# A semaphore for each place of gathered rows, and three and two sets in turn fetched by ScalarE

## The chip, the cores and the metric

The kernel runs on one core of one Trainium2 chip. The metric is the device time of one execution in microseconds (us); of several runs the median counts. The core has five engines with queues of their own: TensorE (PE; its weight loads are PEld), VectorE (DVE), ScalarE (ACT), GpSimd (POOL) and SyncE (SP, which only issues DMAs). Sixteen DMA engines carry out what ScalarE, SyncE and GpSimd issue. An engine works through its queue in order; engines wait for each other, and for DMAs, with semaphores.

## The reference

One layer of a graph network over N = 50,000 nodes with D = 160 features and E = 1,650,000 edges, sorted by destination (every node's edge to itself among them). Each edge takes the features of its source node, combines them with its four edge numbers through five small weight matrices, and adds the result to its destination; then follow two more weight matrices, a ReLU, two residual sums and a layer norm:

```python
s = x[:, :64]
v = x[:, 64:].reshape(n, 32, 3)
ss, vv = (s[src], v[src])
...
out0 = C0 * (ss * e0 @ W1 + dot * INV3 @ W2)
...
m_agg = jax.ops.segment_sum(m, dst, num_segments=n)
...
return x + jax.nn.relu(h)
...
x = _layernorm(x + _L0_gnn_ref(...), axis=-1)
```

Since everything up to the ReLU is linear in the gathered features, the kernel sums first (for each destination, the source rows weighted by each of the four edge numbers) and applies the joined weights once for each block of 128 nodes.

## The kernel before

**Tiling.** The edges are taken in sets of 128, one edge on each partition. Six sets (`G = 6`) make a group whose destinations lie in a window of `W = 32` nodes; two groups (`PG = 2`) make a pair, so a pair has 12 sets; ten pairs (`SG = 20` groups, 120 sets) make a superstep, called `s` in the code. The edges of a node to itself are taken out on the way (by the "packs", lines 594 to 758, of which there are 11) and added from rows read in order, so that 2,087 groups, 12,522 sets in 1,044 pairs and 105 supersteps are left.

**One set.** The 128 source rows of a set, 640 bytes each, come into a tile of 128x160. VectorE builds for a pair the operand `ha` (lines 483 and 486): for each edge a one-hot place in the window, times its four numbers. TensorE multiplies it with the rows (line 511), and the six sets of a group add up in PSUM. VectorE then turns the sums and adds them to a ring of node sums (lines 527 and 536). When a block of nodes is complete, TensorE applies the weights (line 831), VectorE adds the residual and takes mean and variance (lines 186 to 191), ScalarE takes the square root (line 196), VectorE finishes (lines 200 and 202), and SyncE stores. Blocks go two at a time.

**Three ways to get the rows of a set.**

- GpSimd's gather (`gather`, lines 461 to 471): one indirect DMA for a set, with 128 indices from the tile `si`. It writes its place in a tile `xg` of 12 places. The pool has four such tiles (line 235), so 48 places.
- ScalarE's fetches: 128 single DMAs of one row each, whose addresses it loads into registers 32 at a time from `line`, a list that VectorE makes (`list_rows`, lines 403 to 415). From superstep `SCALAR_FIRST = 6` on it fetches two sets of each superstep; the last superstep is left out. Their tiles come from a pool of one more than the largest number a superstep takes.
- SyncE's fetches, one set a superstep from `SYNC_FIRST = 8` on, made in the same way, besides all plain loads and stores.

`spots` (line 359) spreads the fetched sets evenly over a superstep. Their rows are issued in the ten pairs from pair `FBEGIN = 4` of the superstep before to pair 4 of their own, so many after each matmul of the code (`deal`, line 393), and a set is used `FWAIT = 4` pairs after its last row was due to be issued. Each fetched set has a semaphore out of a small ring of them, which its matmul waits for by hand.

**Semaphores of the gathers.** A gather has none by hand. The framework gives the gathers eight semaphores of its own in turn, and makes each gather wait until the one before it on the same semaphore, eight gathers earlier, has landed; the first eight have none to wait for. The first gather of a tile waits besides for the matmuls that read the tile's last contents, four tiles earlier, and has a separate semaphore instruction for what else it waits for. A matmul waits for the semaphore of its own gather.

**Order.** For SyncE, TensorE, VectorE and ScalarE the order is the order of the code (line 1009). In the main loop (lines 1011 to 1063) a pair's gathers are issued first; then come its 12 matmuls, and after the first of them the sums of the pair before are turned, after the third the operand of the next pair is built, and after each the fetchers issue their share and one step of the waiting work (blocks, packs, the next superstep's lists) is taken. The square root of two blocks is so handed over one pair after their sums, and what reads it one pair later. On ScalarE's queue the order is: the rows dealt so far, the square root, the next rows; and a few casts for the packs (lines 613 to 615 and 633).

Of the kernel before, what the change touches and what calls it, by code (L numbers as in the profile page):

```python
# [67 lines left out]
PG = 2  # L68
# [9 lines left out]
KM = WS - 1  # L78
REST = 15
LEAD = 3  # L80
BY_SCALAR, SCALAR_FIRST = (2,), 6
BY_SYNC, SYNC_FIRST = (1,), 8
FBEGIN, FWAIT = 4, 4

def plan(n_nodes, n_edges):

    nblk = 125
    assert n_nodes % nblk == 0
    assert W == FB
    nb = n_nodes // nblk  # L90
    again = 9

    per_unit = P * n_nodes / n_edges
    group = max(g for g in range(1, 17)
                if g == 1 or (g + 0.2) * per_unit + 1 + 5 * math.sqrt(g * per_unit * per_unit / P) <= W)
    head = math.ceil(min(HEAD, n_edges / (group * P)) / SG) * SG
    eh = head * group * P
    row = group * P * 3 // 2 + math.floor(per_unit * group * 3 / 2 * (1 - n_nodes / n_edges))
    assert row * n_nodes / n_edges + 5 * math.sqrt(row * n_nodes / n_edges / 16) < KM

    far = math.ceil(6 * math.sqrt(n_edges) / 2 * n_nodes / n_edges) + 2
    rows = math.ceil((n_edges - eh) / row) + 2
    ngroups = math.ceil((n_edges - n_nodes + eh * n_nodes / n_edges + far) / (group * P))
    assert eh + (rows - 1) * row - n_nodes + eh * n_nodes / n_edges - far >= ngroups * group * P
    units = P * math.ceil(max(math.ceil(n_edges / P) + again - 1, math.ceil((eh + rows * row + 1) / P)) / P)
    return nblk, nb, again, group, units, ngroups, row, head, rows, far
# [3 lines left out]
def tile_gnn_resnorm(ctx: ExitStack, tc: tile.TileContext, x, src, dst, attr, W1, W2, W3, W4, W5, Ws, Wv, out, n_edges):  # L110
    nc = tc.nc
    N = x.shape[0]
    NBLK, NB, GA, G, NU, NG, L, NH, NR, FAR = plan(N, n_edges)
# [95 lines left out]
    def near(g):  # L209
        p = g * G * P  # L210
        return p / degree if p <= EH else EH / degree + (p - EH) / (degree - 1)
# [6 lines left out]
    for g0, g1 in parts:  # L218
        t = min((near(g) / N for g in range(g0, g1 + 1)), key=lambda t: abs(t - 0.5))
# [14 lines left out]
    with tc.tile_pool(name="once", bufs=1) as once, tc.tile_pool(name="raw", bufs=2) as rawp, \  # L234
# [182 lines left out]
        def place(cast_):  # L417
# [40 lines left out]
            begun.append(nc.vector.tensor_reduce(extremes[:, 1, s:s + 1], rel[:, :n], axis=AX.X, op=ALU.max))  # L458
            placed[s] = si, rel, pk[:, :, us]

        def gather(s, placed, u, n):

            xg = rowp.tile([P, PG * G, D], F32, name="xg")
            rows = [fetched.pop((s, u + j), None) for j in range(n)]
            for j in range(n):
                if rows[j] is None:
                    rows[j] = xg[:, j, :], None, None, None
                    nc.gpsimd.indirect_dma_start(  # L468
                        out=xg[:, j, :], out_offset=None, in_=x,
                        in_offset=bass.IndirectOffsetOnAxis(ap=placed[0][:, u + j:u + j + 1], axis=0))  # L470
            return rows

        idle, sent = [], []
# [22 lines left out]
        def fresh(kind):  # L496
            written[kind].append([])

        def wrote(kind, ins):
            ws = written[kind]  # L500
            for old in ws[-3] if len(ws) > 2 else []:
                tc.declare_no_dep(ins.ins, old, reason="its reader has waited for it")
            ws[-1].append(ins.ins)
            return ins

        def group_sums(p, rows, ha):

            ps = psA.tile([P, PG, D], F32, name="ps")
            fresh("ps")
            for j, (xr, sem, count, key) in enumerate(rows):  # L510
                mm = nc.tensor.matmul(ps[:, j // G, :], ha[:, j].rearrange("p k w -> p (k w)"), xr,  # L511
                                      start=j % G == 0, stop=j % G == G - 1)
                if key:
                    mm.wait_op(sem, count, "sem-ge")
                    tc.declare_no_dep(mm.ins, group=key, reason="their own semaphore is waited for")
                    tc.declare_fence(mm.ins, group=key)
                if j % G == 0:
                    wrote("ps", mm)
                else:
                    written["ps"][-1].append(mm.ins)  # L520
                yield ps
# [22 lines left out]
        def row_start(r):  # L544

            lo, hi = (math.floor(r * L * (1 - 1 / degree)) - 2 * FAR - 2, math.ceil(r * L * (1 - 1 / degree)) + 2 * FAR + 2)
            return (max(lo, 0), hi if r else 0), (max(math.floor((EH + r * L) / degree) - FAR - 2, 0),
                                                  math.ceil((EH + r * L) / degree) + FAR + 2)
# [234 lines left out]
        def own_blocks(k):  # L783

            if min((k + 1) * S, N) <= row_start(0)[1][0]:
                return []
            return [list(range(b, min(b + BP, nblocks))) for b in range(k * SB, min((k + 1) * SB, nblocks), BP)]
# [196 lines left out]
        for i in range(npacks):  # L984
# [3 lines left out]
            own = next((k for k in range(NSEG) if min((k + 1) * S, N) > row_start(i * RP)[1][0] and own_blocks(k)), NSEG - 1)  # L988
# [22 lines left out]
        for p, (s, g, ng) in enumerate(pairs):  # L1011
# [5 lines left out]
            if p % per == 0 and s + 1 < NSC:  # L1017
                after_pair(p + 1, do_cast, s + 1)
                after_pair(p + 2, do_place, s + 1)
                if s + 2 == NSC:  # L1020
                    after_pair(p + 4, examine_all)
                    after_pair(p + 6, read_flags)
            rows = gather(s, placed[s], (g - s * SG) * G, ng * G)
            for j, ps in enumerate(group_sums(p, rows, has.pop(p))):
                if j == 1 and turning:
                    turn_sums(*turning)
                    turning = None
                if j == 3 and p + 1 < len(pairs):
                    s1, g1, ng1 = pairs[p + 1]
                    has[p + 1] = spread(placed[s1], (g1 - s1 * SG) * G, ng1 * G)  # L1030
                work(1.0)
                if p % per == FBEGIN and not j:
                    begun_at = p
                    for f in fetchers:
                        f.begin(s)
                for f in fetchers:
                    if f.left:
                        f.deal((p - begun_at + (j + 1) / (ng * G)) / per)
                if packs and p >= START:
                    when = p + (j + 1) / (ng * G)  # L1040
                    todo = math.ceil(len(packs[0]) * min(1, (when - began) / max(1, due[0] - began)))
                    for step in packs[0][done:todo]:
                        if step:
                            step()
                    done = max(done, todo)
                    if done == len(packs[0]):
                        packs.pop(0), due.pop(0)
                        done, began = 0, when
# [35 lines left out]
    with tc.tile_pool(name="up", bufs=1) as up, tc.tile_pool(name="us", bufs=2) as us, tc.For_i(0, once_more, 1):  # L1084
# [3 lines left out]
        mm = up.tile([P, 2, JU], F32, name="mm")  # L1088
# [32 lines left out]
        f = up.tile([PB, CB], F32, name="f")  # L1121
# [12 lines left out]
    with tc.tile_pool(name="edges2", bufs=2) as ep, tc.tile_pool(name="ops2", bufs=2) as op, \  # L1134
            tc.tile_pool(name="node2", bufs=1) as np_, tc.tile_pool(name="psA2", bufs=2, space=PSUM) as psA, \
            tc.tile_pool(name="psF2", bufs=1, space=PSUM) as psF:
        with tc.For_i(0, blocks, 1) as b:
# [5 lines left out]
            with tc.For_i(u0, u1, GA) as u:  # L1143
# [10 lines left out]
                xg = op.tile([P, GA, D], F32, name="xg2")  # L1154
# [71 lines left out]
```

## Time and profile before

| | us |
|---|---|
| median of 3 runs | 15441.45 |
| the runs | 15405.63, 15441.45, 15442.74 |
| the profiled execution, its own time | 15404.57 |
| its span, from the first instruction to the last | 15402.8 |

The granted TensorE clock of the profiled execution is 0.578 of full speed. The queues as the page has them (packets, MB, share of 16 engines):

```profile
q0 software_dynamic: 587040, 1002.66, 27.9%
q1 hardware_dynamic: 266794, 315.98, 6.7%
q10 hardware_dynamic: 51440, 17.04, 0.6%
```

The first is GpSimd's; the 25,088 row fetches of ScalarE and 12,288 of SyncE, and the plain loads and stores, are in the others.

How to read it: a row of the groups has line, engine, operation, what it writes and reads, the count, then busy time in us and the mean ns of one, then the idle time of that engine just before these instructions and what ended most of it. "issue" means that the profile shows nothing that was waited for. Instructions that issue DMAs, load registers or wait for semaphores are not counted as busy, so the share of an engine that mostly issues says little; in a view by time such instructions carry the engine's name with a q (ACTq). A view by time has start, duration, engine, line, operation, and in brackets the idle time before and what ended it. A row of the view of one line's instructions ends with the shortest, median and longest duration in ns and the first and last start in us. A row of a view by stretches has the stretch, its length, then busy time and count of PE, PEld, DVE, ACT and POOL, then the granted clock, the share in which the 16 DMA engines were busy, and GB/s.

### The profile page before, as it was taken

Reading aid. Unit: us, or ns where it says so; the run is one execution under the profiler, and the core shown is the slowest. Engines: PE = TensorE matmul, PEld = TensorE weight load, DVE = VectorE, ACT = ScalarE, POOL = GpSimd, SP = SyncE. Lnnn points to the kernel's source line nnn. Section 1 sums busy time; section 2 is a strip of 40 time slices with the busy share of each in tenths; the row PEclk is TensorE's granted clock in tenths of the full one; section 3 lists DMA queues with packets and bytes.
Section 4 is the critical chain, followed back from the end, with each engine's and each line's share of the span. In section 5 each row is a group of like instructions: output and inputs, shape, how many; then the busy total and the mean of one; then the engine's idle time right before and its main releaser. Section 6 shows DMA issues by size and latency. Waiting matters only on the chain.

```text
span 15402.8 us, 171527 instructions
## 1 busy us (share of the span) xinstructions
PE 10200.3 (66%) x28971; PEld 6755.8 (44%) x28972; DVE 7650.5 (50%) x12616; ACT 171.3 (1%) x273; POOL 11597.4 (75%) x12243
## 2 busy tenths in 40 slices
PE   3666666666666666666666666666666666666666
PEld 3444444444444444444444444444444444444444
DVE  8455355445535543563465355445634553554333
ACT  0000000000000000000000000000000000000000
POOL 7777777777777777777777777777777777777777
PEclk6655555555555555555555555555555555555555
DMA  3333333333333333333333333333333333333333
GB/s 83 100 81 94 91 81 85 97 88 83 92 94 81 84 96 91 81 85 98 87 83 91 93 82 84 97 88 82 86 98 87 81 88 93 81 86 85 86 81 75
DMA packets 906388, 1346.70 MB, mean 87 GB/s; under 512 B 291294, under 2 KB 680162, under 8 KB 902614
## 3 DMA queue, kind: packets, MB, share of 16 engines
q0 software_dynamic: 587040, 1002.66, 27.9%
q1 hardware_dynamic: 266794, 315.98, 6.7%
q10 hardware_dynamic: 51440, 17.04, 0.6%
q14 instruction: 883, 7.23, 0.2%
q8 instruction: 231, 3.78, 0.1%
HBM read 1263.28 MB, written 71.42 MB: 87 GB/s over the span
## 4 chain that ended last, share of the span: by engine, by line
POOL 53%; issue 23%; DMA 19%; PE 5%; DVE 1%; POOLq 0%
POOL xg L468 53%; DMA xg<-in_x,si 19%; PE ps L511 4%; PE phb L831 0%; DVE ha L486 0%; DVE ring L822 0%; DVE ring L536 0%; DVE sums L527 0%; DVE xr L818 0%; DVE hot L483 0%; DVE prow L697 0%; DVE ring L781 0%; DVE pri L692 0%; DVE spots L590 0%; DVE marks L690 0%
## 5 line engine op out<-in xcount | busy, mean ns | idle before, releaser
L468 POOL DMA_INDIRECT xg<-in_x,si x12230 | 11593.9, 948 | 3782.0 <-issue 3511.0
L511 PE MATMUL ps<-xg,ha 128*128 128x160 f32 x24460 | 9452.6, 501 | 5187.1 <-DMA xg<-in_x,si 4721.5
L511 PEld LDWEIGHTS ps<-xg,ha 128*128 128x128 f32 x24460 | 5773.0, 292 | 8629.5 <-DMA xg<-in_x,si 7467.8
L527 DVE STREAM_TRANSPOSE sums<-ps 128x320 f32<-128x320 f32 x1044 | 536.4, 514 | 6840.4 <-PE ps L511 6817.2
L486 DVE TENSOR_TENSOR ha<-hot,pk 128x1536 f32<-128x1536 f32 x1044 | 1830.5, 1753 | 35.9
L831 PE MATMUL phb<-BWk,ring 128*128 128x160 f32 (+1 forms) x3910 | 1256.1, 418 | 0.0
L831 PEld LDWEIGHTS phb<-BWk,ring 128*128 128x128 f32 (+1 forms) x3910 | 1027.4, 296 | 0.0
L536 DVE TENSOR_TENSOR ring<-ring,sums 128x160 f32 x2087 | 684.6, 328 | 340.1 <-issue 203.6
L483 DVE TENSOR_TENSOR hot<-bank,rel 128x384 f32<-128x384 f32 x1044 | 573.4, 549 | 12.6 <-DMA xt<-in_x 10.8
L697 DVE COPY_PREDICATED prow<-marks,prow 128x2370 f32<-128x2370 int32 (+5 forms) x198 | 548.6, 2771 | 1.1
L822 DVE STREAM_TRANSPOSE ring<-xr 128x1280 f32<-128x1280 f32 x188 | 467.4, 2486 | 6.5
L697 DVE COPY_PREDICATED pra<-marks,pra 128x1580 f32<-128x1580 int32 (+5 forms) x198 | 377.0, 1904 | 0.0
L818 DVE TENSOR_TENSOR xr<-xr,bank 128x1280 f32<-128x1280 f32 x188 | 278.9, 1484 | 6.6 <-DVE bank L817 0.2
L186 DVE SCALAR_TENSOR_TENSOR y<-phb,xt 128x320 f32<-128x320 f32 x196 | 95.5, 487 | 240.6 <-PE phb L831 240.3
L196 ACT ACTIVATE rstd<-mv,eps_t 128x2 f32<-128x2 f32 x196 | 58.0, 296 | 14076.2 <-DVE mv L191 13455.5
L533 DVE TENSOR_TENSOR ring<-ring 128x196 f32<-128x196 f32 (+20 forms) x485 | 149.0, 373 | 1.8
L511 PE MATMUL ps<-xscalar,ha 128*128 128x160 f32 x392 | 140.4, 460 | 0.0
L202 DVE TENSOR_SCALAR o<-y,mv,rstd 128x160 f32<-128x160 f32 x391 | 131.3, 377 | 7.5
L694 DVE COPY_PREDICATED_SCALAR hit<-marks,none 128x395 int32 (+5 forms) x198 | 129.8, 656 | 7.0
L781 DVE MEMSET ring<- 128x1280 f32 (+1 forms) x98 | 119.3, 1218 | 22.6 <-issue 22.6
L190 DVE BATCH_NORM_STATS2 st<-y 128x6 f32<-128x160 f32 x391 | 121.7, 311 | 6.7
L695 DVE COPY_PREDICATED hit<-marks,pri 128x395 int32<-128x395 int32 (+5 forms) x198 | 118.2, 597 | 6.9
(352 smaller groups left out, 2173.6 us busy)
## 6 DMA issues: line engine op xcount, KB each, us to landing
xscalar<-in_x ACTq DMA_DIRECT2D x25088, 0.6 KB
xsync<-in_x SPq DMA_DIRECT2D x12288, 0.6 KB
xg<-in_x,si POOLq DMA_INDIRECT x12230
xr<-in_x SPq DMA_DIRECT2D x187, 640.0 KB
r<-edges SPq DMA_DIRECT2D x100, 384.0 KB
edges<-prow SPq DMA_DIRECT2D x1330, 27.8 KB
xt<-in_x SPq DMA_DIRECT2D x195, 160.0 KB
out<-o SPq DMA_DIRECT2D x195, 160.0 KB
```

Source lines behind the costliest of these rows:

```text
L202: nc.vector.tensor_scalar(o[:n, i], y[:n, i], mv[:n, i, 0:1], rstd[:n, i:i + 1], op0=ALU.subtract, op1=ALU.mult)
L468: nc.gpsimd.indirect_dma_start(out=xg[:, j, :], out_offset=None, in_=x, in_offset=bass.IndirectOffsetOnAxis(ap=placed[0][:, u + j:u + j + ...
L483: idle[:] = [nc.vector.tensor_tensor(hot[:, :n], slotsP[:, 0:W].unsqueeze(1).to_broadcast([P, n, W]), rel[:, u:u + n].unsqueeze(2).to_broa ...
L486: nc.vector.tensor_tensor(ha[:, :n], hot[:, :n].unsqueeze(2).to_broadcast([P, n, NK, W]), pk[:, :, u:u + n].rearrange("p k u -> p u k").un ...
L511: mm = nc.tensor.matmul(ps[:, j // G, :], ha[:, j].rearrange("p k w -> p (k w)"), xr, start=j % G == 0, stop=j % G == G - 1)
L527: nc.vector.transpose(at[:, :ng], ps[:, :ng].rearrange("p g (b f) -> p g b f", f=FB))
L533: nc.vector.tensor_tensor(ring[k][:, b, :past], ring[k][:, b, :past], ring[k - 1][:, b, S:S + past], op=ALU.add)
L536: nc.vector.tensor_tensor(here, here, at[:, i], op=ALU.add)
L697: nc.vector.copy_predicated(what[:n, a:e], mi[:, r].unsqueeze(2).to_broadcast([n, e - a, what.shape[2]]), what[:n, a + d:e + d])
L818: nc.vector.tensor_tensor(xr[:, :nq], xr[:, :nq], sumP[:, :nq].unsqueeze(2).to_broadcast([P, nq, D]), op=ALU.mult)
L822: nc.vector.transpose(ring[k][:, :, c0:c0 + nq * W].rearrange("p b (w q) -> p q b w", q=nq), xr[:, :nq].rearrange("p q (b f) -> p q b f", ...
L831: wrote("misc", nc.tensor.matmul(ph[:nb], ring[k][:, i, c0:c0 + nb], BWk[:, i, :], start=i == 0, stop=i == ND - 1))
```

## The change

Two things. First, each of the 48 places (four tiles of 12) gets a semaphore of its own; a gather raises that of its place by 16, the framework's eight are no longer used for gathers, and the matmul that reads the place waits by hand for the count that this gather brings. For the framework's bookkeeping the matmul then stands as the point after which the gather is done. Second, ScalarE fetches three sets of the even supersteps and two of the odd ones, in place of two of each; the pool of its tiles thereby grows from three to four, its ring of semaphores from 12 to 16, and the list that VectorE writes has room for four sets in place of three.

```diff
-BY_SCALAR, SCALAR_FIRST = (2,), 6
+BY_SCALAR, SCALAR_FIRST = (3, 2), 6
...
+        filled = [[tc.alloc_semaphore(f"filled{t}_{j}") for j in range(PG * G)] for t in range(4)]
+        gathers = [[0] * (PG * G) for t in range(4)]
+        begun_tiles = [0]
...
         def gather(s, placed, u, n):
             xg = rowp.tile([P, PG * G, D], F32, name="xg")
             rows = [fetched.pop((s, u + j), None) for j in range(n)]
+            t = begun_tiles[0] % 4
+            begun_tiles[0] += 1
             for j in range(n):
                 if rows[j] is None:
-                    rows[j] = xg[:, j, :], None, None, None
-                    nc.gpsimd.indirect_dma_start(
+                    part = nc.gpsimd.indirect_dma_start(
                         out=xg[:, j, :], out_offset=None, in_=x,
                         in_offset=bass.IndirectOffsetOnAxis(ap=placed[0][:, u + j:u + j + 1], axis=0))
+                    gathers[t][j] += 1
+                    key = f"gather{begun_tiles[0]}_{j}"
+                    part.then_inc(filled[t][j], 16)
+                    tc.no_tile_sem_insts.add(part.ins.name)
+                    tc.add_to_no_dep_group(key, part.ins)
+                    rows[j] = xg[:, j, :], filled[t][j], 16 * gathers[t][j], key
             return rows
...
-                if key:
-                    mm.wait_op(sem, count, "sem-ge")
-                    tc.declare_no_dep(mm.ins, group=key, reason="their own semaphore is waited for")
-                    tc.declare_fence(mm.ins, group=key)
+                mm.wait_op(sem, count, "sem-ge")
+                tc.declare_no_dep(mm.ins, group=key, reason="its own semaphore is waited for")
+                tc.declare_fence(mm.ins, group=key)
```

## The prediction

> **What bounds the kernel now.** I read the page first, then GpSimd's gathers by their line, then GpSimd in order of time, and last ScalarE. The page:
>
> ```profile
> span 15402.8 us, 171527 instructions
> PE 10200.3 (66%) x28971; PEld 6755.8 (44%) x28972; DVE 7650.5 (50%) x12616; ACT 171.3 (1%) x273; POOL 11597.4 (75%) x12243
> ...
> POOL 53%; issue 23%; DMA 19%; PE 5%; DVE 1%; POOLq 0%
> ...
> L468 POOL DMA_INDIRECT xg<-in_x,si x12230 | 11593.9, 948 | 3782.0 <-issue 3511.0
> L511 PE MATMUL ps<-xg,ha 128*128 128x160 f32 x24460 | 9452.6, 501 | 5187.1 <-DMA xg<-in_x,si 4721.5
> ...
> L483 DVE TENSOR_TENSOR hot<-bank,rel 128x384 f32<-128x384 f32 x1044 | 573.4, 549 | 12.6 <-DMA xt<-in_x 10.8
> ```
>
> GpSimd's row is the one to keep: 12,230 gathers, 11,593.9 us busy and 3,782.0 us idle, together 15,375.9 us of a span of 15,402.8. TensorE waits for landings. So GpSimd sets the pace, and the question is what its idle time is. All instructions of the gathers' line, and what they waited for:
>
> ```profile
> L468 POOL DMA_INDIRECT xg<-in_x,si x12230: 940/946/2522, 5.7 to 15379.1; - x198
> L468 POOLq EVENT_SEMAPHORE  x1040: 17/17/43, 58.8 to 15365.4; - x174
> its engine sat idle before it (us, times) until:
>   issue: 3511.0, 11468
>   PE ps L511: 137.6, 445
>   DMA xg<-in_x,si: 121.8, 287
> ```
>
> GpSimd in order of time (start, duration, idle before): the start, a place where it does wait, and its end.
>
> ```profile
> 5.67 1.10 POOL L468 DMA_INDIRECT xg<-in_x,si  x1 [2.89 <-DVE si L426]
> 7.08 0.95 POOL L468 DMA_INDIRECT xg<-in_x,si  x1 [0.31 <-issue]
> 8.33 0.95 POOL L468 DMA_INDIRECT xg<-in_x,si  x1 [0.30 <-issue]
> ...
> 14.58 0.95 POOL L468 DMA_INDIRECT xg<-in_x,si  x1 [0.30 <-issue]
> 15.83 0.95 POOL L468 DMA_INDIRECT xg<-in_x,si  x1 [0.30 <-issue]
> 17.08 0.94 POOL L468 DMA_INDIRECT xg<-in_x,si  x1 [0.30 <-issue]
> ...
> 8399.12 0.95 POOL L468 DMA_INDIRECT xg<-in_x,si  x1 [0.30 <-issue]
> 8402.76 0.94 POOL L468 DMA_INDIRECT xg<-in_x,si  x1 [2.70 <-DMA xg<-in_x,si]
> 8404.18 0.94 POOL L468 DMA_INDIRECT xg<-in_x,si  x1 [0.47 <-DMA xg<-in_x,si]
> ...
> 15379.09 0.95 POOL L468 DMA_INDIRECT xg<-in_x,si  x1 [0.30 <-issue]
> ```
>
> The first eight gathers (5.67 to 14.58) have no earlier gather on their semaphore; the ninth, at 15.83, is the first that must wait for the landing of the one eight before. The step is 1.25 us on both sides of that border. So the 0.30 us is a gather's own price and not a wait; a wait looks like 8402.76, with 2.70 us. The 445 waits put down to TensorE are 137.6 / 445 = 0.31 us each, the ordinary gap: GpSimd never waits for a free place. This also corrects the chain's "DMA 19%": the chain steps through a landing whenever it came shortly before a gather, idle or not.
>
> **The change, part by part.**
>
> *Forty-nine gathers go.* ScalarE fetches for the supersteps 6 to 103. There are 49 even and 49 odd ones: 98 x 2 = 196 sets before, 49 x 3 + 49 x 2 = 245 after, so GpSimd keeps 12,230 - 49 = 12,181. From the first start to the last there are 15379.09 - 5.67 = 15,373.4 us in 12,229 steps, 1.257 us each; an undisturbed step is 1.250. The 49 are worth 61 to 62 us, all on the path that sets the end. I take 61.
>
> *The wait for the gather eight before goes.* With its own semaphore a gather waits for nothing but the matmuls that read its tile four tiles earlier. An ordinary gap is 1.250 - 0.946 (the median gather) = 0.304 us. Idle above that, over all: 3782.0 - 2.9 (before the first gather) - 12,229 x 0.304 = 61 us. Upper bound 61. Lower bound from the waits named as landings alone: 121.8 - 287 x 0.304 = 35 us. Some waits stand under "issue", so I take a value nearer the top, 50. Where does that stall go? The landing stays as late as it was, and TensorE, which waits for it anyway, takes it; GpSimd feels it only when TensorE is 36 places behind, 36 x 1.25 = 45 us. The longest landings of the chain:
>
> ```profile
> 7085.01 9.94 DMA xg<-in_x,si
> ...
> 15369.08 2.55 DMA xg<-in_x,si
> ...
> 15379.09 4.69 DMA xg<-in_x,si
> 15383.78 0.04 issue
> 15383.82 0.90 PE ps L511 x2
> ```
>
> A landing takes 2.55 us at the end, where nobody else fetches, and 9.94 in the middle, which is just the eight steps (10.0 us) that the shared semaphores allow; against 45 us it is nothing.
>
> *GpSimd's separate waits.* 1,040 semaphore instructions of 17 ns stand before the first gather of a tile. Most go: between 0 and 1,040 x 0.017 = 18 us. Since a step with and one without them both come to 1.25 in the rows above, I take 0 and keep 18 for the lower end.
>
> *The matmuls' waits* change their semaphore and not their number: 0.
>
> *ScalarE issues 49 x 128 = 6,272 rows more.* This is the part that can hurt. All its row issues, then ScalarE in time, then the DVE instruction that reads the second square root:
>
> ```profile
> L381 ACTq DMA_DIRECT2D xscalar<-in_x x25088: 227/228/1269, 814.6 to 15214.3; - x200
> ```
>
> ```profile
> 7031.92 54.10 ACTq L381 DMA_DIRECT2D xscalar<-in_x  x128
> 7106.58 0.30 ACT L196 ACTIVATE rstd<-mv,eps_t 128x2 f32<-128x2 f32 x1 [74.44 <-DVE mv L191]
> 7106.65 65.12 ACTq L381 DMA_DIRECT2D xscalar<-in_x  x128
> ```
>
> ```profile
> 7117.80 0.16 DVE L200 RECIPROCAL rstd<-rstd 128x2 f32<-128x2 f32 x1
> ```
>
> A set of 128 rows takes 54.1 us (address loads and register moves included), and then ScalarE stands from 7086.0 to 7106.6 until DVE's variances come. The page's "ACT 1%" hides this: issues are not counted as busy. Fetching lasts 15214.3 - 814.6 = 14,400 us; before, 196 x 54.1 = 10,604 us of it, 74%; after, 245 x 54.1 = 13,255 of about 14,290, 93%. It fits on average but not in each superstep. With three sets ScalarE needs 162.3 us while GpSimd issues 120 - 3 - 1 = 116 gathers in 116 x 1.253 = 145.3 us: it falls 17 us behind. With two it needs 108.2 of 146.6 and catches up. What is queued behind the rows: the square root, read by DVE 7117.80 - 7106.88 = 10.9 us after it is done. A lag of 17 makes DVE wait up to 6 us about once in two supersteps. The operands of the next pair are then late by as much, TensorE starts late, and GpSimd has its 45 us less a landing of 10, that is 35, before it notices. The fetched rows themselves are used four pairs, some 48 gathers or 60 us, after their last issue: 17 us late is hidden. Cost 0; without that cover 49 x 6 = 294 us.
>
> *The DMA engines.* ScalarE now fetches for 93% of the time in place of 74%, so more gathers will have the long landings. Of the 16 DMA engines this is used, from 2,000 to 14,000 us:
>
> ```profile
> 2000.00:14000.00 12000.00, 8042.78 (x22642) 5288.94 (x22642) 6032.41 (x9893) 124.83 (x202) 9046.85 (x9546) 0.57 0.36 88
> ```
>
> Their share is 0.36 at 88 GB/s (the last two columns), and the bytes stay the same: 0. The Trainium skill, page "DMA: Bandwidth & Descriptors", section "Issuing engines are not separate DMA queues", says that DMAs of all issuers interleave on the same 16 engines, and that a second issuer saves issue time only, usually the small part. The trace agrees with the first half (2.55 against 9.94 us) and differs in the second: here the issue, 1.25 us a gather, is the bound.
>
> *VectorE* makes one more clipped row of 128x32 in each even superstep; at the 549 ns of its 128x384 compare, 49 x 0.55 = 27 us of an engine that is half idle: 0.
>
> **The sum.** Of the profiled execution: 15,402.8 - 61 - 50 = 15,292 us of span; built up again, 5.67 + 12,180 x (0.948 + 0.305) + (15402.8 - 15379.1) = 15,291. The execution took 15,404.57, 1.8 more than its span: 15,294. The three runs shown are 15,405.63, 15,441.45 and 15,442.74: the profile lies by the lowest of them, and the median 37 above it. Where those 37 us come from no view shows; if from late landings they go too. I add a third of it: **15,305 us**.
>
> **The rivals.**
>
> *The landings hold GpSimd in another place.* With up to 48 gathers open instead of eight, the room for their descriptors could run out, and the wait would stand inside the gather. For it: the longest gather took 2,522 ns beside a median of 946. Against: the mean of 948 leaves 12,230 x 0.002 = 24 us for all of that, and TensorE stays close behind the landings, so few are open. Only the 61 us remain: 15,402.8 - 61 + 1.8 = 15,344, or 15,381 beside the median. The same figure holds if the framework keeps the old waits, so that the semaphores do not do what they say. (The Trainium skill, same page, section "SWDGE vs HWDGE vs iDMA", says that GpSimd writes descriptors to rings in a carved-out part of SBUF; how full they are no run here shows.)
>
> *The moved rows slow the gathers that stay.* A moved set still uses the same DMA engines, and if landings grew until TensorE was 36 places behind, the 61 us of issue would be given back as waits for places: 15,294 + 61 = 15,355. (That is how the rule just named would speak against the change.) For it: landings already stretch fourfold beside the rows. Against: they would have to reach 45 us at a DMA share of 0.36.
>
> *ScalarE's lag reaches GpSimd.* The 6 us of DVE's wait pass through in a third of the cases: about 100 us of 294, 15,305 + 100 = 15,405, no change. Against: the 35 us of slack.
>
> *ScalarE becomes the bound: slower.* The path is ScalarE's queue from 814.6 on. Outside the fetching lie 15,402.8 - 14,400 = 1,003 us. The point from which it decides is 14,400 / 245 = 58.8 us a set; below it the kernel is not slower for it. For it: the second set above took 65.1, and rows issued beside a busier DMA may take longer than 228 ns (the longest 1,269). Against: in those 65.1 is a wait for DVE's list, and a whole set stands at 54.1. Midway, at 59.6, it is 1,003 + 245 x 59.6 = 15,605 us, and DVE, then TensorE, then GpSimd follow ScalarE.
>
> **How the numbers follow.** The forecast 0.78, landings elsewhere 0.09, slowed gathers 0.02, lag reaching GpSimd 0.05, ScalarE the bound 0.06. The forecast's low end: gains of 62 + 61 + 18 from 15,404.6 give 15,264; its high end takes the 35 and the whole 37: 15,404.6 - 61 - 35 + 37 = 15,346. The first rival's 15,381 is taken in: 15,265 to 15,385. A run is told from no change at 0.3%, 46 us (below 15,395): faster 0.90 (forecast, the first two rivals, and a part of the third), same 0.04, slower 0.06.
>
> **What would show it.** Right: 12,181 gathers; their idle time near 12,181 x 0.305 = 3,715 us, with no row of waits for landings; first to last start near 12,180 x 1.253 = 15,261 us; 31,360 rows of ScalarE; a square root now and then late, DVE's wait for it under 10 us. Wrong in the second part: a longer mean gather than 948 ns, or waits for TensorE well over 0.31 us each. Wrong about ScalarE: a set that takes 59 us or more with no wait in it, ScalarE without pauses before the square roots, and DVE waiting tens of us for them.

## The result, and the profile after

| | us |
|---|---|
| the changed kernel, median of 4 runs (15337.86 to 15347.95) | 15341.79 |
| the kernel before, median of 4 runs (15405.63 to 15442.74) | 15436.44 |
| the changed kernel's profiled execution, its own time | 15340.96 |
| its span | 15339.1 |

The ratio is 0.994, with a 95% interval of 0.9927 to 0.9953: faster by 0.6%, 95 us. The forecast was 15,305 in a range of 15,265 to 15,385. The page of the changed kernel, its head and the two groups that stand against those of before (now on lines 473 and 522):

```profile
span 15339.1 us, 182899 instructions
...
PE 9998.2 (65%) x28971; PEld 6683.8 (44%) x28972; DVE 7656.0 (50%) x12665; ACT 171.7 (1%) x273; POOL 11588.2 (76%) x12194
...
L473 POOL DMA_INDIRECT xg<-in_x,si x12181 | 11584.7, 951 | 3722.2 <-issue 3591.6
L522 PE MATMUL ps<-xg,ha 128*128 128x160 f32 x24362 | 9236.8, 496 | 5305.4 <-DMA xg<-in_x,si 4585.4
```

All instructions of the gathers' line in the changed kernel:

```profile
L473 POOL DMA_INDIRECT xg<-in_x,si x12181: 942/949/2522, 5.7 to 15310.1; - x200
...
  issue: 3591.6, 11766
  PE ps L522: 118.5, 384
```

GpSimd still sets the pace: 11,584.7 + 3,722.2 = 15,306.9 us of 15,339.1. The gathers' rows of before and after and the end behind the last gather give the whole difference of the spans, 63.7 us. Idle time fell by 3782.0 - 3722.2 = 59.8 us: 49 x 0.305 = 15 belong to the gathers that are gone, and 45 to the waits. No row "DMA xg" is left among what GpSimd waited for, the longest "issue" wait is 0.3 us, an ordinary gap, and 118.5 / 384 = 0.31 us is an ordinary gap too. Busy time should have fallen by 49 x 0.948 = 46 us and fell by 9.2: the mean gather took 951 ns in place of 948, and 12,181 x 3.06 ns give 37 us back. (The 3.06 are the means before rounding, 951.05 and 947.99.) The gaps between gathers, counted one by one in the two traces, say the same of the waits: before, 120 of them are longer than 0.35 us and hold 51 us above the ordinary 0.305; after, two are, and they hold 2.4 us (one near the start, which before has too, and the one of 1.56 us shown below). After the last gather came 15,339.1 - 15,310.1 = 29 us in place of 23.7, 5 more. Together -61 - 45 + 37 + 5 = -64.

ScalarE, in order of time, and what VectorE and TensorE waited for, in the changed kernel:

```profile
7011.21 0.30 ACT L196 ACTIVATE rstd<-mv,eps_t 128x2 f32<-128x2 f32 x1 [90.68 <-PE ps L522]
7011.29 80.62 ACTq L381 DMA_DIRECT2D xscalar<-in_x  x192
7091.95 0.30 ACT L196 ACTIVATE rstd<-mv,eps_t 128x2 f32<-128x2 f32 x1 [80.44 <-PE ps L522]
7092.03 69.40 ACTq L381 DMA_DIRECT2D xscalar<-in_x  x167
7161.48 0.29 ACT L196 ACTIVATE rstd<-mv,eps_t 128x2 f32<-128x2 f32 x1 [69.23 <-issue]
```

```profile
POOL xg L473 <- issue: 3591.6, 11766, 0.3
...
PE ps L522 <- DVE ha L497: 575.8, 59, 45.6
...
DVE sa L826 <- DMA sa<-selves: 381.7, 27, 43.5
...
DVE hit L644 <- ACT marks L643: 242.4, 24, 30.5
...
POOL xg L473 <- PE ps L522: 118.5, 384, 1.6
...
DVE rstd L200 <- ACT rstd L196: 43.6, 14, 10.8
```

The same view of the kernel before has for the first three:

```profile
PE ps L511 <- DVE ha L486: 87.2, 6, 36.4
...
DVE hit L634 <- ACT marks L633: 51.5, 12, 30.3
...
DVE sa L816 <- DMA sa<-selves: 21.7, 7, 9.0
```

Each of these rows gives the total in us, the number of waits, and the longest. In the stretch shown ScalarE goes from its rows to the square root and back without a pause: 7011.29 + 80.62 = 7091.91, and the root starts at 7091.95. Of the 177 roots between 1,300 and 15,100 us, 86 have less than 0.5 us before them; before the change none had, and the median pause was 18.7 us. The 192 rows of a stretch with three sets took 80.6 us. VectorE waits for ScalarE's casts (line 643, before 633) 242 us in place of 52, and for its square roots (line 196) 44 us in place of none. It also waits 382 us in place of 22 for the self shares that SyncE loads, and TensorE 576 in place of 87 for its operands; how much of these two comes from ScalarE's lag no view shows. At GpSimd next to nothing arrives: its longest wait for TensorE is 1.6 us. That one wait shows how large the cover is:

```profile
1844.92 0.19 DVE L826 TENSOR_TENSOR sa<-sa,bank 128x32 f32<-128x32 f32 x1 [43.48 <-DMA sa<-selves]
...
1864.34 4.07 PE L522 MATMUL ps<-xg,ha 128*128 128x160 f32 x14 [45.55 <-DVE ha L497]
...
1870.59 0.96 POOL L473 DMA_INDIRECT xg<-in_x,si  x1 [1.56 <-PE ps L522]
```

VectorE stood 43.5 us for a load, TensorE in its train 45.6 us for its operand, and GpSimd 1.56 us, or 1.26 more than the ordinary gap, for a place. So 48 places cover a stop of TensorE of about 45 us, as the forecast had worked out (36 places of 1.25 us), and this stop just used them up.

### The profile page after: what moved, and what is told of

Same layout as the page of the kernel before. It is cut to its first block, busy times and chain, and to the rows that moved or that the text cites. A ratio compares the mean times of both kernels' runs of the same rounds, so it can differ in the third digit from the quotient of the medians.

```text
span 15339.1 us, 182899 instructions
## 1 busy us (share of the span) xinstructions
PE 9998.2 (65%) x28971; PEld 6683.8 (44%) x28972; DVE 7656.0 (50%) x12665; ACT 171.7 (1%) x273; POOL 11588.2 (76%) x12194
## 5 line engine op out<-in xcount | busy, mean ns | idle before, releaser
L473 POOL DMA_INDIRECT xg<-in_x,si x12181 | 11584.7, 951 | 3722.2 <-issue 3591.6
L522 PE MATMUL ps<-xg,ha 128*128 128x160 f32 x24362 | 9236.8, 496 | 5305.4 <-DMA xg<-in_x,si 4585.4
L522 PEld LDWEIGHTS ps<-xg,ha 128*128 128x128 f32 x24362 | 5688.8, 289 | 8616.2 <-DMA xg<-in_x,si 7920.1
L522 PEld LDWEIGHTS ps<-xscalar,ha 128*128 128x128 f32 x490 | 137.2, 314 | 0.0
```

Source lines behind the costliest of these rows:

```text
L473: part = nc.gpsimd.indirect_dma_start(out=xg[:, j, :], out_offset=None, in_=x, in_offset=bass.IndirectOffsetOnAxis(ap=placed[0][:, u + j:u ...
```

## The experiments

The experiments stand in four groups, each on a chip of its own together with runs of the kernel before. On all four chips the kernel before took 20,870 to 21,040 us (medians), a third more than in the runs above. So each kernel is compared only with the kernel before of its own group, and what made these executions longer became a question of its own.

**The two parts, and both kernels again.** `e1` is the kernel before, `e4` the changed one. `e2` is the changed kernel with

```diff
-BY_SCALAR, SCALAR_FIRST = (3, 2), 6
+BY_SCALAR, SCALAR_FIRST = (2,), 6
```

and `e3` the kernel before with

```diff
-BY_SCALAR, SCALAR_FIRST = (2,), 6
+BY_SCALAR, SCALAR_FIRST = (3, 2), 6
```

> The kernel before, unchanged, with a profile on the chip on which the next three run. Its three runs lay at 15,405.6, 15,441.5 and 15,442.7 us, and its profiled one (15,404.6) had a median gather of 946 ns; the changed kernel's had 949 in all parts of the run, the first gathers included. Theory A (a gather's price differs between executions or chips by 3 ns, whatever the kernel; 12,230 x 3 ns = 37 us, which is just the distance between the runs of before): this run's median gather is the same as that of the changed kernel beside it, 949 with a time near 15,440, or 946 with one near 15,405. Theory B (a gather with a semaphore of its own, or without a wait, takes 3 ns longer): here 946, and the runs at 15,440 stay unexplained.

> The 48 semaphores, with ScalarE at two sets in every superstep as before: 12,230 gathers. Theory: only the waits for the gather eight before go, 35 to 61 us, about 45: GpSimd's idle time falls from 3,782 to about 3,737 us, and no wait for a landing is left. Time against the kernel before on the same chip: 15,440 - 45 = 15,395 (ratio 0.997) under theory A; under theory B the longer gather (12,230 x 3 = 37 us) takes nearly all of it back, and the time is within 10 us of before. Rival (the landings hold GpSimd elsewhere): the idle time does not fall, or the waits for TensorE grow by as much.

> ScalarE with three and two sets, and the eight semaphores as before: 12,181 gathers. Theory: 49 x 1.257 = 62 us less than before; the waits for landings stay, and may grow a little, as more gathers run beside ScalarE's rows (35 to 80 us over the ordinary gap in place of 35 to 61). Time 15,440 - 62 = 15,378 (ratio 0.996). Rival (ScalarE's lag reaches GpSimd): waits for TensorE over 0.31 us each on GpSimd, and a time over 15,400. Under theory B the median gather is 946 here and 949 in the run of the semaphores alone; under A both are the same.

> The changed kernel again, beside the three others. If the parts add up: before less about 45 less 62, that is 15,440 - 107 = 15,333, ratio 0.993. Theory A: its median gather is that of the kernel before in this call.

| | us | ratio to the kernel before on the same chip | median gather, ns |
|---|---|---|---|
| `e1` before | 20,879 | 1.0006 (0.9983 to 1.0028) | 949 |
| `e2` semaphores alone | 20,876 | 0.9994 (0.9971 to 1.0016) | 949 |
| `e3` three and two sets alone | 23,219 | 1.112 (1.108 to 1.117) | 949 |
| `e4` both | 23,149 | 1.110 (1.106 to 1.114) | 946 |

Here the change makes the kernel 11% slower, all of it by the fetches. The kernel before, ScalarE in time and its rows' durations:

```profile
9019.18 0.30 ACT L196 ACTIVATE rstd<-mv,eps_t 128x2 f32<-128x2 f32 x1 [98.02 <-issue]
9021.60 98.59 ACTq L381 DMA_DIRECT2D xscalar<-in_x  x128
9120.24 0.30 ACT L196 ACTIVATE rstd<-mv,eps_t 128x2 f32<-128x2 f32 x1 [100.76 <-issue]
```

```profile
L381 ACTq MOVE xscalar<-in_x x25088: 1/29/1733, 1032.1 to 20799.7; - x200
L381 ACTq DMA_DIRECT2D xscalar<-in_x x25088: 1/235/1688, 1032.2 to 20799.7; - x200
```

The changed kernel has for the register moves in its first profile:

```profile
L381 ACTq MOVE xscalar<-in_x x31360: 29/29/38, 817.1 to 15146.1; - x200
```

A register move that took 29 to 38 ns there takes up to 1.7 us here. The median row is nearly the old one, but every so often instructions come 0.7 us, or a multiple of it, apart. The set shown takes 98.6 us in place of 54.1. That is above the 58.8 us at which ScalarE becomes the bound, and even in the kernel before ScalarE has no pause before the square roots. What VectorE waited for before it used the square root (line 200), and GpSimd before its gathers, in the kernel before:

```profile
  ACT rstd L196: 6462.1, 135
```

```profile
POOL xg L468 <- PE ps L511: 4398.6, 360, 56.9
```

and in the changed kernel beside it:

```profile
  ACT rstd L196: 9498.4, 156
```

```profile
POOL xg L473 <- PE ps L522: 6739.9, 379, 77.0
```

The lag goes the way that the rival gave it: ScalarE, VectorE, TensorE, GpSimd, which now waits for free places up to 77 us. From the first row to the last it takes 20,799.7 - 1,032.1 = 19,768 us for 196 sets, 101 us a set with all of ScalarE's work, and in `e4` 23,068.3 - 1,032.1 = 22,036 us for 245, 90 us. So the price of a set is not a constant of these executions: the 49 sets more cost 2,268 us, 46 each.

The semaphores alone do not change the time: GpSimd mostly waits for free places here, and the semaphores do not bring those sooner. The kernels with eight semaphores (`e1`, `e3`, and `e6`, `e9`, `e11` below) have 23 to 30 waits that the profile puts down to a landing, 7 to 10 us in all and so hardly more than ordinary gaps; none of the kernels with 48 has any. On the price of a gather, a median of 949 ns comes here with the kernel before and 946 with the changed one, the other way round than in the first profiles, and `e2` and `e3` both have 949. Theory B falls. Of theory A only one form holds: the price is the execution's. It is not the chip's, as the expectations of `e1` and `e4` also had it.

**The two parts again, on a second chip,** with the same kernels:

> The 48 semaphores alone, ScalarE at two sets, once more, since in the first four runs ScalarE's and SyncE's instructions came in steps of 0.7 and 1.4 us thousands of times, so that a set of rows took 91 us in place of 54 and ScalarE was the bound there (over the 58.8 us a set of the forecast) for the kernel before too. What the runs of before will show by themselves: if the kernel before takes about 15,440 us here, the rows are back at 54 us a set, and this kernel should take 15,440 - 45 = 15,395 (ratio 0.997), with GpSimd's idle time about 45 us less and no wait for a landing. If the kernel before takes 20,900 again, ScalarE is the bound, and the semaphores change nothing (ratio 1.000), as in the first run of it.

> ScalarE with three and two sets, the eight semaphores as before, once more. If the kernel before takes about 15,440 us here: 62 us less, 15,378 (ratio 0.996), with the same median gather as the run beside it. If it takes 20,900: ScalarE is the bound, its 31,360 rows against 25,088 set the end, and the ratio is 1.11 again.

Before 21,039 us; the semaphores alone 21,027 (ratio 0.9989, 0.9964 to 1.0013), the fetches alone 23,350 (1.109, 1.103 to 1.115). The result is the same. The semaphores alone now have a median gather of 946 ns, the fetches alone 949.

**Fewer rows on ScalarE, on a third chip.** `e7` is the changed kernel with

```diff
-BY_SCALAR, SCALAR_FIRST = (3, 2), 6
+BY_SCALAR, SCALAR_FIRST = (1,), 6
```

and `e8` the semaphores alone once more.

> The 48 semaphores, and one set of each superstep on ScalarE in place of three and two: 98 sets, 12,544 rows, and 12,230 + 98 = 12,328 gathers. Theory (the end is set by whichever of two queues is longer: GpSimd with 1.253 us a gather, ScalarE with its sets): GpSimd needs 12,328 x 1.2535 + 29 = 15,482 us. Where the kernel before takes 20,900 to 21,000 (a set at 91 us), ScalarE now has 98 x 91 = 8,900 us and no longer counts: 15,480 to 15,600, a quarter less than before. Where the kernel before takes 15,440 (a set at 54 us), this one is slower by 98 x 1.2535 = 123 less the 45 of the semaphores: 15,440 + 78 = 15,518, ratio 1.005. Rival where before takes 20,900 (SyncE, whose instructions come in the same steps, or something else of that state holds all engines, not ScalarE's count of rows): the time stays over 19,000.

> The 48 semaphores alone, ScalarE at two sets, a third time. If the kernel before takes about 15,440 us here: 15,395 (ratio 0.997), idle time of GpSimd about 45 us less than before and no wait for a landing. If it takes 20,900: ratio 1.000 again.

`e7` took 19,612 us against 20,907 (0.939, 0.935 to 0.942); `e8` 20,870 (0.9988, 0.9969 to 1.0007). With half of the rows of before on ScalarE the time is 6% less, although GpSimd has 98 gathers more, so ScalarE's rows weighed on the end. But the rest of my expectation was wrong: 15,480 to 15,600 was forecast, and the rival, over 19,000, came true. What `e7` waited for:

```profile
POOL xg L473 <- PE ps L522: 2878.8, 254, 74.3
DVE sa L826 <- DMA sa<-selves: 2389.9, 90, 100.6
...
PE ps L522 <- DMA xsync<-in_x: 489.5, 16, 59.2
```

VectorE waits for the loads that SyncE issues, and TensorE for SyncE's row fetches. SyncE issues one set a superstep as before, and now its queue is the late one.

**No rows at all, or one set, with eight or 48 semaphores, on a fourth chip.** `e9` and `e11` are the kernel before, `e10` and `e12` the changed one; in all four SyncE fetches nothing (`BY_SYNC = (0,)`), and ScalarE nothing in `e9` and `e10`, whose new lines follow, and one set in the other two (`BY_SCALAR = (1,)`):

```diff
+BY_SCALAR, SCALAR_FIRST = (0,), 6
+BY_SYNC, SYNC_FIRST = (0,), 8
```

> No row fetches by ScalarE or SyncE, the framework's eight semaphores: 12,522 gathers. Meant to make GpSimd the bound also where the kernel before takes 20,900 us. Theory (there the row fetches of ScalarE and SyncE are what is slow): GpSimd's queue alone sets the end, 12,522 x 1.2535 + 29 = 15,725 us, plus at most 20 of waits for landings, since without rows a landing takes about 2.6 us. Against 20,900 that is a quarter less; against 15,440 it is 1.9% more. Rival (something else is slow there): the time stays over 18,000.

> No row fetches, the 48 semaphores: 12,522 gathers, 15,725 us. Theory: the semaphores are worth the waits for late landings and nothing else, so here, where landings are early, within 20 us of the kernel with eight. Rival (a gather that waits for nothing is cheaper or dearer by itself): a difference of the mean gather or of the ordinary gap, 12,522 times.

> ScalarE fetches one set a superstep, SyncE none, eight semaphores: 12,522 - 98 = 12,424 gathers. Theory: a moved set is worth one step of GpSimd, 98 x 1.253 = 123 us less than without fetches, 15,602, less what waits for landings come in again beside ScalarE's rows (up to 40 us). Rival (the DMA engines, or rows in the slow steps, give it back): over 15,680.

> ScalarE one set, SyncE none, the 48 semaphores: 12,424 gathers and no wait for a landing: 15,602 us. Theory: less than the kernel with eight semaphores by the sum of its waits for landings above the ordinary gap (10 to 40 us).

| | gathers | us | ratio to before (20,906 us) |
|---|---|---|---|
| `e9` none, eight semaphores | 12,522 | 17,936 | 0.857 (0.854 to 0.860) |
| `e10` none, 48 | 12,522 | 17,935 | 0.857 (0.854 to 0.860) |
| `e11` one set, eight | 12,424 | 17,926 | 0.857 (0.854 to 0.860) |
| `e12` one set, 48 | 12,424 | 17,918 | 0.857 (0.854 to 0.860) |

All four end together, 2,200 to 2,300 us above what GpSimd's gathers need (15,602 to 15,725). With 98 gathers less the time falls by 11 to 16 us and not by 123. So GpSimd is not the bound here either, and the theory that the row fetches alone are slow falls. What GpSimd waited for in `e9` ("remote" is a releaser that the profile does not find on this core), the group of TensorE's matmuls, and some of them in order of time:

```profile
POOL xg L468 <- PE ps L511: 1583.7, 282, 35.7
POOL xg L468 <- remote: 729.3, 191, 7.2
```

```profile
L511 PE MATMUL ps<-xg,ha 128*128 128x160 f32 x25044 | 6528.1, 392 | 10503.1 <-issue 9515.1
```

```profile
9028.16 0.43 PE L511 MATMUL ps<-xg,ha 128*128 128x160 f32 x1 [2.38 <-issue]
9030.25 0.43 PE L511 MATMUL ps<-xg,ha 128*128 128x160 f32 x1 [1.67 <-issue]
9030.95 0.43 PE L511 MATMUL ps<-xg,ha 128*128 128x160 f32 x1 [0.27 <-issue]
9031.65 0.43 PE L511 MATMUL ps<-xg,ha 128*128 128x160 f32 x1 [0.27 <-issue]
9032.35 3.94 PE L511 MATMUL ps<-xg,ha 128*128 128x160 f32 x17 [0.27 <-issue]
```

The starts lie 2.1, 0.7, 0.7 and 0.7 us apart, with nothing that the profile shows to wait for. TensorE's idle time before these matmuls is 10,503 us, 9,515 of it "issue", where the kernel before had 5,187 in its first profile, nearly all of it for landings. TensorE's matmuls stand on the same 0.7 us step as ScalarE's register moves. GpSimd's two waits make 2,313 us, about what lies above its own need. The comparison of eight and 48 semaphores that these four were made for can't be had from them: GpSimd waits for TensorE, and TensorE is held in these steps.

**What the steps have in common.** In the trace of `e1` the queues step together. Counted by microsecond, with a step being a distance of two instruction starts within 25 ns of a multiple of 0.695 us: where ScalarE came in such steps and SyncE issued too, SyncE came in them as well in 97% of the time; where ScalarE kept its ordinary pace, in 28%. So one thing seems to hold both queues at once. What it is, no run shows; that the recording of the instructions itself holds the queues is a rival that no run here rules out.

## Why the prediction was right

**The bound.** GpSimd's gathers set the end in the runs that the forecast was for, with 0.30 us of gap at each gather, which the new semaphores did not take away. 11,140 of the changed kernel's gathers wait for nothing (all but one a tile), and their gap is the same 0.305: the reading of the first eight gathers held.

**Forty-nine gathers, 61 us.** Right, by count and price.

**The waits for late landings, 50 us, between 35 and 61.** It was 45 by the sum of the idle time and 49 by the long gaps, all of them gone, and 1.26 us came back as a wait for a place. This is read from the two first profiles; in the eight traces of kernels with 48 semaphores no wait is put down to a landing. A run with the semaphores alone in which GpSimd is the bound was not had, so the split of the 95 us between the two parts is read and not shown by an experiment of its own.

**Separate waits, matmuls' waits, DMA engines, VectorE: 0.** Right as far as GpSimd's idle time shows. The separate semaphore instructions fell from 1,040 to 104. The rows that the forecast showed hold no step with such an instruction, but the trace bears its reading out: the gathers on both sides of the first one start at 58.67 and 59.91 us, 1.24 apart. The Trainium skill's rule that spoke against the change (page "DMA: Bandwidth & Descriptors", section "Issuing engines are not separate DMA queues": issuers share the DMA engines and save issue time only) did not decide: GpSimd waited for a place 1.6 us at most, so the moved rows held no gather back. What the study's runs add to it is that the second issuer's own issue time can count: in `e1`, at 101 us a set, ScalarE had less than 0.5 us of pause before 163 of the 165 square roots between 1,300 and 19,000 us.

**ScalarE's lag, cost 0.** Right, with the cover that was named: 192 rows took 80.6 us, as 1.5 x 54.1 = 81 had it, the square roots were late, and VectorE waited for them 43.6 us in 14 waits. The longest was 10.8 us, where 6 was forecast and under 10 was named as a sign of being right. ScalarE without pauses before the square roots, named as a sign of being wrong, came at half of them and did no harm by itself. What the prediction had not named cost VectorE more: the packs' casts on ScalarE's queue, 242 us, and SyncE's loads of the shares, 382 us. TensorE's waits for operands grew to 576 us, and the 48 places covered them; the longest, 45.6 us, they just covered. That it was not longer was luck, since the forecast had counted on stops of 6 us.

**What failed: "Where those 37 us come from no view shows; if from late landings they go too. I add a third of it".** The price of a gather was taken from one profile, where the median was 946 ns. In the changed kernel's it was 949, from the first gathers on, before ScalarE fetches anything. A mean gather longer than 948 ns was also the forecast's sign that the waits had moved into the gather, its first rival. The traces speak against that: the median itself moved, and by the same 3 ns through the whole run, and the kernel before has 946 in its first profile and 949 in `e1`, the changed one 949 and, in `e4`, 946. So it is the execution's and not the change's. 12,230 x 3 ns = 37 us is also the distance between the two kinds of times of the kernel before. With the whole 37 the forecast would have been 15,294 + 37 = 15,331, 11 us below the measured median; the end after the last gather, 5 us longer, is half of that, and the waits, 45 in place of 50, the other half. That the runs of before at 15,431 to 15,443 us had gathers of 949 ns fits, but they left no trace, so it is argued. It would also explain why the gain is 95 us between the medians and only 64 between the two profiles: the profile of before is of its fastest run.

**The rival "ScalarE becomes the bound".** It had 0.06, and lost in the runs forecast for: a set stayed at 54 us. In the kernels of this study with two and three sets it is what happens, beyond the point that it gave (58.8 us a set, 90 to 101 measured) and along the path that it gave. Its sum does not hold: with the 101 us of `e1` it would give 1,003 + 245 x 101 = 25,748 us for the changed kernel, and `e4` took 23,149. The forecast took 54.1 us as a property of the kernel; it differs between executions, and in the longer ones with the number of sets too.

## What to carry to other kernels

Work that is moved from a bound queue to a queue that is then 93% full is a gain only as long as the second queue's price holds; work out the price at which the sign turns, and see how far the trace is from it. Before a wait is priced, compare the step with and without it: the first instructions on a ring of semaphores have none to wait for. And where one instruction comes 12,000 times, 3 ns of it are as large as the effect that is looked for: compare its median in both profiles before a difference is put down to the change.

## What was not expected of the hardware

- A gather of 128 rows took 946 or 947 ns (median) in some executions and 949 in others, the whole run through, whatever the kernel and on the same chip (`e3` 949 and `e4` 946, on one chip). What sets it stays open.
- In all runs of this study instructions of ScalarE, SyncE and TensorE came at times in steps of 0.7 us and its multiples, register moves as well as DMA issues and matmuls; GpSimd's gathers kept their step of 1.25 us wherever they waited for nothing. The kernel before then takes 20,870 to 21,040 us in place of 15,436. Fewer row fetches help (`e7` 0.939, `e9` to `e12` 0.857 of the kernel before), which shows that these queues set the end, but not what holds them; that they step together in `e1` (97% against 28%) speaks for one cause. In that condition the kernel without any row fetches beats both kernels; in the other, by GpSimd's step, it would take 12,522 x 1.2535 + 29 = 15,725 us and lose to both, which was not run there.
